# Gathered pairs added at every fourth unit of products, and count groups stored without gaps, in a three-layer graph kernel

## The chip, the cores and the metric

The kernel runs on one core of one Trainium2 chip. The metric is device time in microseconds (us), the median over runs of the same program. A profile is one further execution, with every instruction and every DMA packet recorded.

## What is computed

The input is a graph of 2500 nodes with 256 features each and 80000 edges (src, dst), sorted by dst. After a layer norm and a relu come three layers of edge convolution, and their outputs, joined, go through one more matrix:

```python
def _edge_conv(x, src, dst, W, b):
    xi = x[dst]
    xj = x[src]
    m = jnp.concatenate([xi, xj - xi], axis=-1) @ W + b
    s = jax.ops.segment_sum(m, dst, num_segments=N)
    cnt = jax.ops.segment_sum(jnp.ones((dst.shape[0],), m.dtype), dst, num_segments=N)
    return s / jnp.maximum(cnt, 1.0)[:, None]
...
h = jnp.maximum(_layernorm(x, axis=-1), 0.0)
xs = [h]
for W, b in ((W0, b0), (W1, b1), (W2, b2)):
    h = jax.nn.relu(_edge_conv(h, src, dst, W, b))
    xs.append(h)
return x + jnp.concatenate(xs, axis=-1) @ Wf + bf
```

The sum over the edges of a node can be written as a product with a matrix of counts: entry (s, d) is the number of edges from node s to node d. The kernel builds that matrix on the chip and multiplies with it, once per layer.

## The kernel before, in words

The nodes lie in NT = 20 tiles of 128. The columns of the count matrix (the destination nodes) are cut into windows of W = 6 nodes, and the windows into NG = 5 groups: four of 80 windows (480 columns) and a last one, group 4, of 78 windows (468 columns). FEW = 112 destination nodes, which fit in no window, are treated apart, by gathering their edges' rows one by one.

**The count groups.** One group is a tile `a` of 128 partitions x 20 node tiles x 480 columns (`new_a`, L796), in one of two pools, by the group's parity. So two groups at a time are in the on-chip memory. In layer 0, `build` (L835) fills a group from compared keys while the products of the group before run; `finish` (L847) then stores it to `a_dram[g]` in DRAM. Group 4 uses 468 of the tile's 480 columns, so that each of its 20 rows in a partition is followed by a gap of 48 bytes, on the chip and in DRAM, and its store (L850) and its load (L856) move 20 rows of 1872 bytes per partition. The other groups have no gap. Layers 1 and 2 load with `load_a` (L853) the groups that are no longer there.

**Layers 1 and 2** (L1054 to L1090). First `nodes_split` (L754) makes `z`, the node features times a part of the weights, as a high and a low half (`zh`, `zl`) for TensorE and as a whole in DRAM (`z_dram`). Then the five groups follow, in the order 4, 3, 2, 1, 0 in layer 1 and 0 to 4 in layer 2. For each group:

- `final` (L778) is called for the node tiles that the group touches: products with a part of Wf into one of four PSUM banks, and one VectorE addition into `acc`.
- `layer` (L932) yields after each of its 24 units of TensorE work, u = 0 to 23: 20 units of four products of `zh` or `zl` with the counts (L947), and then four units of own products (L951). ScalarE takes the result at the end (L954).
- After the group, `load_a` is called for the group two places further in the order, into the buffer that has just been read. So there are three loads in each layer, and group 4 is loaded once, in layer 2, after the third group, for use as the fifth.

**The gathered pairs.** For the FEW nodes, 60 gathers per layer fetch 128 rows of `z_dram` each, with an index per partition. `gather_pairs` (L902) is a generator over k = 0 to 33. Step k issues the two gathers of pair k on GpSimd's queue, into one of four buffers (`room`, L885), and adds pair k - 4 to `sums` on VectorE. The addition of pair k - 4 stands behind the gathers of that pair, and pair k + 1 can only be gathered once that addition has freed a buffer. The first call runs k = 0 to 3; each later `next(few)` runs one k.

Before the change, `next(few)` is called at the units u = 4, 6, ..., 18 of each group (L1079): eight per group, k = 4 to 11 in the first one. The 30 steps are used up in the fourth group.

**What sets the order.** Engines run side by side, but each runs its own instructions in the order of the program (helpers whose names end in "o" keep that order, and are all recorded at L280). A `next(few)` inside a group thus puts its addition on VectorE behind the `final` additions of that group and ahead of those of the next one. On GpSimd's queue the gathers share the order with the additions of x to `acc` (`add_rest`, L768, layer 1 alone). The loads stand on SyncE's queue (SP).

Of the kernel before, what the change touches and what calls it, by code (L numbers as in the profile page):

```python
# [8 lines left out]
F32 = mybir.dt.float32  # L9
# [256 lines left out]
F32R = mybir.dt.float32r  # L266
# [20 lines left out]
def run(it):  # L287
    for _ in it:
        pass
# [22 lines left out]
def by_windows(ctx: ExitStack, tc: tile.TileContext, x, src, dst, Ws, bs, Wf, bf, out, missing):  # L312
    nc = tc.nc
    PE, DVE, ACT, POOL, SP = nc.tensor, nc.vector, nc.scalar, nc.gpsimd, nc.sync
    PEo, DVEo, POOLo, ACTo, SPo = (InOrder(tc, e) for e in (PE, DVE, POOL, ACT, SP))
    P = 128
    N, D = x.shape
    E = src.shape[0]
    NT = (N + P - 1) // P
# [5 lines left out]
    W = 6  # L325
# [17 lines left out]
    GWS = []  # L343
    while sum(GWS) < NW:
        GWS.append(min(80, NW - sum(GWS)))
    G = max(GWS) * W
    GS = 480
    NG = len(GWS)
# [11 lines left out]
    dram = ctx.enter_context(tc.tile_pool(name="wdram", bufs=1, space=DRAM))  # L360
# [39 lines left out]
    cnt_few = const.tile([P, FEW], F32R, name="cnt_few")  # L400
    mine = const.tile([P, W], F32, name="mine")
    most = const.tile([P, 1], F32, name="most")
    a_dram = [dram.tile([P, NT, G], F32, name=f"a_dram{g}") for g in range(NG)]

    apools = [ctx.enter_context(tc.tile_pool(name="apool0", bufs=1))]
    pre = ctx.enter_context(ExitStack())
# [25 lines left out]
    def load_wb(l, queue=SP):  # L432
        ws[l] = wpool.tile([P, DC, D], F32, name="wt"), wpool.tile([P, DC, D], F32, name="wb", bufs=1)
        queue.dma_start(ws[l][1], Ws[l][D:2 * D, :].rearrange("(c p) d -> p c d", p=P))

    def load_wt(l, queue=SP):
        queue.dma_start(ws[l][0], Ws[l][0:D, :].rearrange("(c p) d -> p c d", p=P))

    def load_wf(l, queue=SP):
        wfs[l] = wpool.tile([P, DC, D], F32, name="wf", bufs=1)  # L440
        queue.dma_start(wfs[l], Wf[l * D:(l + 1) * D, :].rearrange("(c p) d -> p c d", p=P))
# [22 lines left out]
    def load_b(l, queue=SP):  # L464
        queue.dma_start(brow[PAD:PAD + 1, l % 2, :], bs[l].rearrange("(o d) -> o d", o=1))
# [288 lines left out]
    def nodes_split(l, t, zf):  # L754
        pz = bank()
        for c in range(DC):
            PE.matmul(pz[:, :D], hT[:, c, t * P:(t + 1) * P], ws[l][1][:, c, :],  # L757
                      start=(c == 0), stop=(c == DC - 1))
        sc = share[:, t:t + 1]
        if t == NT - 1:  # L760
            DVEo.scalar_tensor_tensor(zf, pz[:, :D], sc, brow[:, l % 2, :], op0=OP.mult, op1=OP.add)
        else:
            ACT.activation(zf, pz[:, :D], AF.Copy, scale=sc)
        SPo.dma_start(z_dram[l][t * P:(t + 1) * P, :], zf)
        DVEo.tensor_copy(zh[:, t, :], zf)
        DVEo.tensor_sub(zl[:, t, :], zf, zh[:, t, :].bitcast(F32))

    def add_rest(ts):  # L768

        a, b = ts[0], ts[-1] + 1  # L770
        DVEo.tensor_add(acc[:, a:b, :], acc[:, a:b, :], bf_sb.unsqueeze(1).to_broadcast([P, b - a, D]))
        yield
        full = min(b, NT - 1)
        POOLo.dma_start(acc[:, a:full, :], xr[:, a:full, :], accum_op=OP.add)
        if b == NT:
            POOLo.dma_start(acc[:LAST, NT - 1, :], x[(NT - 1) * P:N, :], accum_op=OP.add)

    def final(l, t):  # L778
        po = bank()
        for c in range(DC):  # L780
            PE.matmul(po[:, :D], hT[:, c, t * P:(t + 1) * P], wfs[l][:, c, :],  # L781
                      start=(c == 0), stop=(c == DC - 1))
        DVEo.scalar_tensor_tensor(acc[:, t, :], po[:, :D], share[:, t:t + 1], acc[:, t, :], op0=OP.mult, op1=OP.add)
        if l == L:
            n = P if t < NT - 1 else LAST
            SP.dma_start(out[t * P:t * P + n, :], acc[:n, t, :])


    def group_of(g):
        return FEW + sum(GWS[:g]) * W, GWS[g] * W  # L790

    def touched(g):
        c0, n = group_of(g)
        return [t for t in range(NT) if (t + 1) * P > c0 and t * P < c0 + n]

    def new_a(g):  # L796
        return apools[g % 2].tile([P, NT, GS], F32R, name="a")

    windows = [(g, s, min(BW, GWS[g] - s)) for g in range(NG) for s in range(0, GWS[g], BW)]
    ones_of = {}  # L800
# [46 lines left out]
    def finish(g, a):  # L847
        c0, n = group_of(g)
        ACTo.copy(a[PAD:PAD + 1, NT - 1, :n], cnt[PAD:PAD + 1, c0:c0 + n])
        SP.dma_start(a_dram[g][:, :, :n], a[:, :, :n].bitcast(F32))  # L850
        yield

    def load_a(g):  # L853
        a = new_a(g)
        n = group_of(g)[1]
        SP.dma_start(a[:, :, :n].bitcast(F32), a_dram[g][:, :, :n])  # L856
        return a

    def by_count(g):
# [20 lines left out]
    def add_sums(n):  # L880
        while n > 1:
            n //= 2
            DVEo.tensor_add(sums[:, :n, :], sums[:, :n, :], sums[:, n:2 * n, :])
# [6 lines left out]
    def rooms(l):  # L890

        for _ in range(AHEAD):
            two = room()
            yield two[:, 0, :]
            yield two[:, 1, :]
        for i in range(SUMS):
            yield sums[:, i, :]
        for _ in range(AHEAD):
            yield hot.tile([P, BW * CH, NB], BF16, name="one_n", bufs=AHEAD).rearrange(
                "p k m -> p (k m)")[:, :2 * D].bitcast(F32)  # L900

    def gather_pairs(l):  # L902

        got = []
        for k in range(EDGES // 2 + PAIRS):
            if k >= PAIRS:
                if k == PAIRS + 1:
                    DVEo.tensor_add(sums[:, :2, :], got[0], got[1])
                elif k > PAIRS:
                    DVEo.tensor_add(sums[:, :2, :], sums[:, :2, :], got[k - PAIRS])  # L910
            if k < EDGES // 2:
                two = room()
                got.append(two)
                for i in range(2):
                    POOLo.indirect_dma_start(
                        out=two[:, i, :], out_offset=None, in_=z_dram[l][:, :],
                        in_offset=bass.IndirectOffsetOnAxis(ap=who[:, 2 * k + i:2 * k + i + 1], axis=0))
            if k >= PAIRS - 1:
                yield
# [12 lines left out]
    def layer(l, g, a, own, PE=PE, ACT=ACT):  # L932

        c0, n = group_of(g)
        pa = ps_agg.tile([P, DC, 512], F32, name="pa")
        ways = [(o, c) for o in range(DC) for c in range(DC)]
        units = [(0, k) for k in range(NT)]
        for i, u in enumerate(own):
            units.insert(u + i, (1, i))
        last = {}  # L940
        for kind, i in units:
            last.update({o: (kind, i, o) for o in (range(DC) if kind == 0 else ways[i][:1])})
        for kind, i in units:
            if kind == 0:
                for o in range(DC):
                    for z in (zh, zl):
                        PE.matmul(pa[:, o, :n], z[:, i, o * P:(o + 1) * P], a[:, i, :n],  # L947
                                  start=(i == 0 and z is zh), stop=(z is zl and last[o] == (kind, i, o)))
            else:
                o, c = ways[i]  # L950
                PE.matmul(pa[:, o, :n], ws[l][0][:, c, o * P:(o + 1) * P], hT[:, c, c0:c0 + n],  # L951
                          start=False, stop=(last[o] == (kind, i, o)))
            yield
        ACT.activation(hT[:, :, c0:c0 + n], pa[:, :, :n], AF.Relu)  # L954
# [8 lines left out]
    a = new_a(0)  # L963
# [55 lines left out]
    for g in range(NG):  # L1019
# [26 lines left out]
        if g + 1 < NG:  # L1046
            run(finish(g + 1, a1))
            held, a = a, a1
# [5 lines left out]
    for l in range(1, L):  # L1054
        groups = list(range(NG))
        if l % 2:
            groups.reverse()


        last = [t for t in touched(groups[0]) if t]  # L1060
        for t, zf in zip([t for t in range(1, NT) if t not in last] + last + [0], rooms(l)):
            nodes_split(l, t, zf)
        few = gather_pairs(l)
        next(few)
        if l + 1 < L:
            load_b(l + 1)
            load_wb(l + 1)
            load_wt(l + 1)
        finished = []
        for j, g in enumerate(groups):  # L1070
            now = [t for t in touched(g) if t not in finished]
            for t in now:
                final(l, t)
            finished += now
            rest = add_rest(now) if l == 1 else None
            if j == NG - 1:
                load_wf(l + 1)
            for u, _ in enumerate(layer(l, g, tiles[g], LATE)):
                if 4 <= u < NT and u % 2 == 0:  # L1079
                    next(few, None)  # L1080
                if rest and u in (1, NT):
                    next(rest, None)
            if j == 1 and l + 1 < L:
                DVEo.tensor_sub(ws[l + 1][0], ws[l + 1][0], ws[l + 1][1])
            if j + 2 < NG:
                del tiles[g]
                tiles[groups[j + 2]] = load_a(groups[j + 2])
        run(few)
        add_sums(2)
        layer_few(l)  # L1090
# [41 lines left out]
```

## Time and profile before

| | |
|---|---|
| median of 3 runs | 551.21 us (550.27 to 553.93) |
| the profiled execution, its own time | 549.29 us |
| its span, first to last instruction | 547.6 us |
| TensorE busy | 511.1 us, 93% of the span |
| VectorE, ScalarE, GpSimd busy | 263.9, 136.3, 261.3 us |
| mean granted TensorE clock | 0.964 |
| gathers of pairs (`one_m<-z_dram,who`) | 120, 979 ns each on GpSimd |
| additions of pairs (`sums<-sums,one_m`) | 56, 692 ns each; 118.8 us of waiting for gathers before them |
| loads of a count group (`a<-a_dram`) | five of 4800 KB, one of 4680 KB |

PE is TensorE, PEld its weight loads, DVE VectorE, ACT ScalarE, POOL GpSimd, SP SyncE. In the chain of waits, each row is a start, a length and the work (or the wait) that held up the end of the kernel. "issue" is time in which the engine waited for nothing that the profile shows. The granted clock is the share of its full rate that TensorE was given.

The stages in the span: preparation to 61 us, layer 0 with the building of the counts to 205 us, layer 1 to 357 us, layer 2 to 524 us, the last `final` products to the end.

### The profile page before, as it was taken

The numbers are of one execution on the slowest core, as the hardware profiler recorded it, in microseconds if no ns is written. First come the engines' busy times: TensorE is split into PE (matmuls) and PEld (weight loads), VectorE is DVE, ScalarE is ACT, GpSimd is POOL, SyncE is SP. The second block draws the span as 40 slices with busy tenths as digits, with TensorE's granted clock in tenths as the row PEclk, the third lists the DMA queues.
The fourth block names the chain that finished last, engine by engine and source line by source line (L and its number), as shares of the span: only waits on it lengthen the run. The fifth ranks groups of instructions, "written<-read, shape, count | busy, mean of one in ns | idle before, by whom it ended". The sixth has DMA issues, their size and how long they took to land.

```text
span 547.6 us, 7491 instructions
## 1 busy us (share of the span) xinstructions
PE 511.1 (93%) x2875; PEld 415.1 (76%) x2875; DVE 263.9 (48%) x556; ACT 136.3 (25%) x310; POOL 261.3 (48%) x243
## 2 busy tenths in 40 slices
PE   8999999999999999994999999999939999984996
PEld 4888887888888888882778787788817787854875
DVE  7999888898888126621332122356213231211033
ACT  6666675547343205100000000042000000000000
POOL 4782278878788800277564534002762755400000
PEclk9999999999999999996899999999968999996999
DMA  8238759979996597333989999523337588994023
GB/s 277 70 97 156 132 220 304 395 112 342 144 274 181 87 271 255 111 105 102 368 267 300 143 344 120 91 96 116 105 105 310 171 261 201 181 154 160 1 78 115
DMA packets 42547, 100.29 MB, mean 183 GB/s; under 512 B 4663, under 2 KB 36870, under 8 KB 41350
## 3 DMA queue, kind: packets, MB, share of 16 engines
q1 hardware_dynamic: 22310, 68.78, 33.4%
q0 software_dynamic: 19264, 29.84, 32.7%
q10 hardware_dynamic: 928, 1.11, 0.7%
q8 instruction: 24, 0.39, 0.3%
q14 instruction: 21, 0.17, 0.1%
HBM read 62.21 MB, written 37.50 MB: 182 GB/s over the span
## 4 chain that ended last, share of the span: by engine, by line
PE 85%; DMA 9%; issue 4%; DVE 1%; ACT 0%; SPq 0%; DVEq 0%; ACTq 0%
PE pa L947 29%; PE pa L280 20%; PE bank L781 9%; PE bank L280 9%; DMA a<-a_dram 7%; PE bank L757 6%; PE pz L280 6%; PE pa L951 5%; DMA wf<-in_L_gnn_Wf_dram 2%; PE turned L280 1%; DMA dst_i<-in_dst_dram 1%; DVE one_n L280 0%; DVE one_m L280 0%; ACT hT L280 0%; DVE acc L280 0%
## 5 line engine op out<-in xcount | busy, mean ns | idle before, releaser
L280 POOL DMA_INDIRECT one_m<-z_dram,who x120 | 117.5, 979 | 150.0 <-DVE acc L280 65.4
L947 PE MATMUL pa<-a,zh 128*128 128x480 f32 (+1 forms) x400 | 156.1, 390 | 11.8 <-DMA a<-a_dram 9.4
L947 PE MATMUL pa<-a,zl 128*128 128x480 f32 (+1 forms) x400 | 153.8, 385 | 0.4 <-issue 0.4
L280 POOL DMA_INDIRECT sums<-z_dram,who x60 | 100.2, 1670 | 25.3 <-issue 17.1
L280 DVE TENSOR_TENSOR sums<-sums,one_m 128x512 f32<-128x512 f32 x56 | 38.8, 692 | 123.0 <-DMA one_m<-z_dram,who 118.8
L947 PEld LDWEIGHTS pa<-a,zh 128*128 128x128 f32 x400 | 76.7, 192 | 25.5 <-issue 12.9
L947 PEld LDWEIGHTS pa<-a,zl 128*128 128x128 f32 x400 | 76.6, 192 | 13.2 <-issue 0.9
L280 PE MATMUL pa<-a,zh 128*128 128x480 f32 (+1 forms) x200 | 81.6, 408 | 0.0
L280 DVE TENSOR_TENSOR one_m<-iota_m,key_m 128x1024 bf16<-128x1024 bf16 x100 | 68.8, 688 | 17.5 <-PE bank L280 15.4
L954 ACT ACTIVATE hT<-pa 128x960 f32<-128x960 f32 (+1 forms) x10 | 9.7, 968 | 271.2 <-PE pa L951 205.5
L280 PE MATMUL pa<-a,zl 128*128 128x480 f32 (+1 forms) x200 | 75.8, 379 | 0.0
L280 DVE SCALAR_TENSOR_TENSOR acc<-bank,share,acc 128x256 f32<-128x256 f32 x60 | 27.5, 481 | 81.2 <-PE bank L781 81.2
L280 ACT CAST a<-bank 128x480 fp32r<-128x480 f32 x100 | 51.4, 564 | 58.9 <-PE bank L280 53.9
L280 DVE TENSOR_TENSOR one_n<-iota_n,key_n 128x960 bf16<-128x960 bf16 x100 | 65.2, 652 | 0.0
L781 PE MATMUL bank<-wf,hT 128*128 128x256 f32 x240 | 56.5, 387 | 9.0 <-issue 8.5
L781 PEld LDWEIGHTS bank<-wf,hT 128*128 128x128 f32 x240 | 46.6, 194 | 18.9 <-issue 12.5
L280 PEld LDWEIGHTS <-one_m 128*128 128x128 bf16 x796 | 43.3, 98 | 8.9 <-issue 3.3
L280 PE MATMUL bank<-one_n,one_m 128*128 128x120 bf16 x796 | 49.0, 216 | 0.2 <-ACT junk L280 0.2
L280 PEld LDWEIGHTS pa<-a,zh 128*128 128x128 f32 x200 | 37.7, 188 | 8.5 <-issue 3.0
L951 PE MATMUL pa<-hT,wt 128*128 128x480 f32 (+1 forms) x80 | 37.7, 605 | 6.8 <-issue 6.8
L280 PEld LDWEIGHTS pa<-a,zl 128*128 128x128 f32 x200 | 37.6, 188 | 7.0 <-issue 2.1
L757 PE MATMUL bank<-wb,hT 128*128 128x256 f32 x160 | 34.9, 379 | 0.0
(145 smaller groups left out, 413.3 us busy)
## 6 DMA issues: line engine op xcount, KB each, us to landing
a<-a_dram SPq DMA_DIRECT2D x5, 4800.0 KB
a_dram<-a SPq DMA_DIRECT2D x4, 4800.0 KB
a_dram<-a SPq DMA_DIRECT2D x1, 4680.0 KB
a<-a_dram SPq DMA_DIRECT2D x1, 4680.0 KB
out_dram<-acc SPq DMA_DIRECT2D x19, 128.0 KB, 1.7
z_dram<-one_m SPq DMA_DIRECT2D x16, 128.0 KB, 3.4
z_dram<-sums SPq DMA_DIRECT2D x16, 128.0 KB, 3.6
acc<-in_x_dram POOLq DMA_DIRECT2D x4, 512.0 KB
```

Source lines behind the costliest of these rows:

```text
L280: return self.tc.keep_in_program_order(call(*args, **kwargs))
L757: PE.matmul(pz[:, :D], hT[:, c, t * P:(t + 1) * P], ws[l][1][:, c, :], start=(c == 0), stop=(c == DC - 1))
L781: PE.matmul(po[:, :D], hT[:, c, t * P:(t + 1) * P], wfs[l][:, c, :], start=(c == 0), stop=(c == DC - 1))
L947: PE.matmul(pa[:, o, :n], z[:, i, o * P:(o + 1) * P], a[:, i, :n], start=(i == 0 and z is zh), stop=(z is zl and last[o] == (kind, i, o)))
L951: PE.matmul(pa[:, o, :n], ws[l][0][:, c, o * P:(o + 1) * P], hT[:, c, c0:c0 + n], start=False, stop=(last[o] == (kind, i, o)))
L954: ACT.activation(hT[:, :, c0:c0 + n], pa[:, :, :n], AF.Relu)
```

## The change

Three places, and no other line:

```diff
-    a_dram = [dram.tile([P, NT, G], F32, name=f"a_dram{g}") for g in range(NG)]
+    a_dram = [dram.tile([P, NT, n * W], F32, name=f"a_dram{g}") for g, n in enumerate(GWS)]
...
     def new_a(g):
-        return apools[g % 2].tile([P, NT, GS], F32R, name="a")
+
+        n = group_of(g)[1]
+        a = apools[g % 2].tile([P, NT * GS], F32R, name="a")
+        return a[:, :NT * n].rearrange("p (t n) -> p t n", n=n)
...
-        SP.dma_start(a_dram[g][:, :, :n], a[:, :, :n].bitcast(F32))
+        SP.dma_start(a_dram[g], a.bitcast(F32))
...
     def load_a(g):
         a = new_a(g)
-        n = group_of(g)[1]
-        SP.dma_start(a[:, :, :n].bitcast(F32), a_dram[g][:, :, :n])
+        SP.dma_start(a.bitcast(F32), a_dram[g])
         return a
...
             for u, _ in enumerate(layer(l, g, tiles[g], LATE)):
-                if 4 <= u < NT and u % 2 == 0:
+                if u % 4 == 1:
                     next(few, None)
```

For groups 0 to 3 the tile and its place in DRAM are what they were. In group 4 a row of 468 columns now follows the one before it directly, so a partition holds 37440 bytes in one piece. `next(few)` is now called at u = 1, 5, 9, 13, 17 and 21: six per group, k = 4 to 9 in the first, and the 30 steps are used up exactly at u = 21 of the fifth group.

## The prediction

> **What bounds the kernel now.** I read the page first: TensorE is busy for 93% of the span, and the chain is TensorE for 85%, a DMA for 9%, "issue" for 4%.
>
> ```profile
> span 547.6 us, 7491 instructions
> ...
> PE 511.1 (93%) x2875; PEld 415.1 (76%) x2875; DVE 263.9 (48%) x556; ACT 136.3 (25%) x310; POOL 261.3 (48%) x243
> ...
> PE 85%; DMA 9%; issue 4%; DVE 1%; ACT 0%; SPq 0%; DVEq 0%; ACTq 0%
> ```
>
> So only time in which TensorE stands can be won. The chain in order of time says where it stands:
>
> ```profile
> 249.12 1.56 issue
> 250.68 0.38 PE bank L781
> 251.05 1.78 issue
> ...
> 261.11 0.82 issue
> 261.93 19.28 PE pa L947 x80
> ...
> 397.68 1.56 issue
> ...
> 442.83 17.59 PE pa L947 x80
> 460.44 39.30 DMA a<-a_dram
> 499.74 0.14 issue
> 499.87 19.28 PE pa L947 x80
> ```
>
> Three places. Place C is the load of group 4 in layer 2, issued at 460.44, landed at 499.74; the waits say "PE pa L947 <- DMA a<-a_dram: 9.4". Places A (249.1 to 261.9, layer 1) and B (397.7 to about 413.3, layer 2) are no wait for data: TensorE goes on, but its instructions come singly, 0.7 to 2.8 us apart, with "issue" between. The busy times by stretch show both sides:
>
> ```profile
> core 0: us, PE busy (x) PEld busy (x) DVE busy (x) ACT busy (x) POOL busy (x), PEclk, DMA share, GB/s
> 227.90:248.50 20.60, 20.60 (x91) 16.94 (x90) 5.91 (x8) 0.00 (x0) 15.72 (x17) 1.00 0.34 96
> 248.50:262.00 13.50, 4.18 (x10) 2.16 (x9) 0.69 (x1) 0.00 (x0) 9.86 (x10) 0.62 0.43 106
> ...
> 413.50:428.00 14.50, 14.50 (x62) 12.10 (x62) 4.61 (x8) 0.97 (x1) 6.22 (x6) 0.93 0.93 375
> 443.00:459.00 16.00, 16.00 (x75) 13.66 (x74) 4.33 (x8) 0.91 (x1) 8.12 (x8) 1.00 0.94 335
> 460.40:499.90 39.50, 30.09 (x126) 23.09 (x124) 9.36 (x18) 1.94 (x2) 11.37 (x12) 0.93 0.90 182
> ```
>
> Ten products in the 13.5 us of A, 91 in the 20.6 us before. The loads of whole rows (413.5 and 443) move 375 and 335 GB/s, with gathers beside them; the load with gaps only 182 with gathers beside it.
>
> What do A and B share? GpSimd's timeline: in both, the first group's stream of gathers, back to back at 1.25 us.
>
> ```profile
> 227.91 0.99 POOL L280 DMA_INDIRECT one_m<-z_dram,who  x1 [36.39 <-DVE acc L280]
> ...
> 257.12 0.94 POOL L280 DMA_INDIRECT one_m<-z_dram,who  x1 [0.30 <-issue]
> ...
> 379.33 1.08 POOL L280 DMA_INDIRECT one_m<-z_dram,who  x1 [29.02 <-DVE acc L280]
> ...
> 408.34 0.95 POOL L280 DMA_INDIRECT one_m<-z_dram,who  x1 [0.30 <-issue]
> ```
>
> Each stream has 24 gathers (pairs 0 to 11). A ends 3.9 us after the last of them (261.9 against 258.06), B 4.0 us after (413.3 against 409.29). The beginnings are less alike, at gather 17 in A and 15 in B. The later stream of 16, from 420 to 440, shows no such place (20.50 us of TensorE in 20.50). I take the stalls to hang on a long stream of gathers and to end with it. That is an inference from two cases; the profile names no releaser.
>
> **The skill.** "DMA: Bandwidth & Descriptors", section "Queues, rings and completion order", says that each DMA engine goes round its queues a packet at a time. That agrees with place C: between 466 and 492, with gathers running, all DMA moves 163 GB/s, and from 493, after the last gather, 307. One short row of 1872 bytes per turn, against a gather's packet, is a poor share; a whole row per turn is a good one. "TensorE: Matmul & The Clock Gate", section "Part 1: The HAM clock gate", says that an idle window of about 3.4 us takes TensorE to half rate until a busy window has passed. The trace agrees: the clock is 0.62 in A, and the 80 products after C take 19.28 us against 17.04 for the same shapes at 227.64. I found no page on instructions that come 0.7 us apart. "SBUF — State Buffer", section "Operand start alignment", allows any fp32 start at a multiple of four bytes and times none.
>
> **The change, part by part.** *1. Load without gaps.* It removes the wait of 9.41 us and the half-clock restart, 19.28 - 17.04 = 2.24: **11.65 us**. The cover: TensorE needs group 4 at 490.47 (499.87 - 9.41), 30 us after the issue. 4680 KB are 4.79 MB; at the slower of the two rates, 335 GB/s, that is 14.3 us, landed by 475; at half of that rate it would still land at 489. The wait is back below 4.79 MB / 30.0 us = 160 GB/s. The gathers beside it lose: the pairs of the fourth group stand behind whole rows for some 15 us, as at 445.52 to 459.72, where VectorE waits 12.28 us for a pair. What is late next is VectorE; it must be through the additions of one group when TensorE comes to the `final` of the group after the next, since four banks carry the four `final` tiles between. That is a group, 24 us, of lag; the largest before is 323.86 - 308.68 = 15 us. So it is covered. The store in layer 0 (184.7) has no reader before layer 2: nothing.
>
> *2. Shape of the group's rows.* The 80 products of group 4 in each layer read rows that begin at multiples of 1872 instead of 1920 bytes. No row of the trace shows it. Best 0; worst, an estimate, a tenth of 3 x 17.04 = 5 us. A gain has no reason. I take 0.
>
> *3. Fewer additions per group.* Same 60 gathers at 979 ns and the same additions at 692 ns; none is on the chain, so moving them costs nothing directly while TensorE covers them. Of what they pass: on POOL, at u = 21, one pair follows layer 1's x addition, two DMAs at most, 2.44 us; on DVE, the step at u = 1 now stands ahead of the bias addition (1.49 us at most), for which only that x addition waits, and nothing of layer 1 reads its result. SP's queue is not touched. The last group had no pair and gets six: four have been gathered, two more cost 4 x 1.25 us and some 3 us to land; they begin at about 337 in layer 1 and are added by 348, before the few nodes' products at 357; layer 2 has 30 us. Covered.
>
> *4. The stream of the first group.* Six steps instead of eight: 20 gathers, 4 x 1.25 = 5.0 us shorter. If A and B end with it, each is 5.0 us shorter, less what TensorE did in that time: in A about 2.5 products of 0.22 (0.5 us), in B about 2.8 of 0.40 (1.1 us). Gain 4.5 + 3.9 = **8.4 us**. Bounds: 0, if the stalls have another cause, and all of it. In A: 13.2 us with seven products' worth of 1.5, and 1.7 of half clock after it (19.28 against 17.57), so 13.4. In B, 397.3 to 414.6, 17.3 us, with 3.6 of work: 13.7. Together 27 us.
>
> Sum on the profiled execution: 549.29 - 11.65 - 8.4 = 529.2. The median of the runs lies 1.9 above that execution: **531.1 us**.
>
> **Rivals.** *The stalls are not the gathers'.* Two stalls only, with beginnings at different gathers, and 60 gathers in layer 0 without one (at 1.67 us, with accumulation) speak for it; the ends speak against. Then only 11.65: 539.6 us. *They go altogether*, if the stall needs more than some 20 gathers, or the pairs that pile up unadded after the last addition of the group. The stall at gather 15 to 17 speaks against. 551.21 - 11.65 - 27.1 = 512.5 us. *The load is not joined* into one piece per partition: 551.21 - 8.4 = 542.8 us. Against it: the loads of 480 columns, written as three dimensions too, already run at 335 to 392 GB/s. *Slower:* the stall counts gathers in flight, and gathers held behind a whole-row load count. Every one of the eight later groups now has a stream of 12; with one stall of 3.2 us in each, 25.6 us, against at most 20.05 won, the time is 551.21 - 20.05 + 25.6 = 556.8. It decides from 20.05 / 8 = 2.5 us per group. Against it: streams of 16 beside loads show nothing before.
>
> **How the numbers follow.** Both parts as summed 0.42; stalls as before 0.27; stalls gone 0.15; load not joined 0.06; slower 0.06; the remaining 0.04 for a wait that only moves, near no change. I give the time of the first. The likeliest one's own range is 524 to 536 (5 us for the row starts above, some 7 for a half clock that falls otherwise or a stall that begins later below). For 8 in 10 the range reaches from the stalls gone to the load not joined: 512 to 544. What a measurement of this kernel can tell is 1%, 5.5 us: faster is all below 545.7. That takes the first four cases, 0.90; no change 0.05; slower 0.05.
>
> **What would show it.** In the profile of the changed kernel: the load of group 4 in layer 2 lands within 20 us and TensorE has no wait on it (step 1); the products of 468 columns stay at 0.21 us apart (step 2); no `sums` wait reaches the few nodes' products (step 3); the first streams have 20 gathers, and the "issue" places end about 4 us after them (step 4). I am wrong if the places A and B keep their length, or if TensorE waits for VectorE's `acc` additions.

## The result and the profile after

The changed kernel takes 532.48 us (median of 4 runs, 531.97 to 533.3) against 551.47 us beside it: ratio 0.965, 95% interval 0.962 to 0.969. The prediction was 531.1 us. The sum came out right, and four of its terms did not: one cost was missed, two gains were mis-sized, and one gain, seen in later runs alone, was held to be nothing.

The page of the changed kernel, its span, its busy times and its chain:

```profile
span 531.6 us, 7489 instructions
...
PE 506.9 (95%) x2875; PEld 414.1 (78%) x2875; DVE 264.6 (50%) x556; ACT 136.0 (26%) x310; POOL 268.9 (51%) x243
...
PE 66%; POOL 14%; DMA 14%; issue 4%; DVE 1%; ACT 0%; SPq 0%; POOLq 0%; ACTq 0%
```

GpSimd is now in the chain with 14%, and it was not there before. The waits of TensorE tell why:

```profile
PE pa L280 <- DVE sums L280: 9.1, 1, 9.1
PE pa L953 <- issue: 4.5, 5, 1.5
...
PE bank L781 <- issue: 1.5, 2, 0.9
PE pa L949 <- issue: 0.7, 2, 0.3
```

The wait of 9.4 us for the load of group 4 is gone, and the "issue" waits of places A and B are down from 8.5 + 6.8 + 2.7 = 18.0 us to 6.7. The same lines before:

```profile
PE bank L781 <- issue: 8.5, 6, 1.8
PE pa L951 <- issue: 6.8, 6, 2.4
PE pa L947 <- issue: 2.7, 3, 1.6
```

But a wait of 9.1 us for `sums` is new: it is the few nodes' product at the end of layer 0. (Lines of the changed kernel stand two lower: L949 is the L947 of before.) The chain in order of time, from the end of layer 0 through place A:

```profile
193.50 17.73 DMA sums<-z_dram,who
...
213.72 2.47 PE pa L280 x10
216.19 18.36 PE bank L757 x80
234.55 4.32 PE bank L781 x20
238.87 17.00 PE pa L949 x80
...
261.17 0.59 issue
261.75 0.47 PE bank L781
262.23 0.92 issue
...
264.56 17.62 PE pa L949 x79
```

The last gather of layer 0 took 17.73 us to land. Layer 1's first product starts at 238.87, and started at 227.64 before. Place A is there still, but only from 261.2 to 264.6. Cut at the same products, the two spans compare so (us, worked out from the starts of the groups' products; the columns on the right are a later pair of profiles, `e9_before` and `e8_after`, taken on two chips and told of below):

| stretch | before | after | difference | before, later run | after, later run | difference |
|---|---|---|---|---|---|---|
| to the first product of layer 1 | 227.64 | 238.87 | +11.23 | 231.94 | 237.67 | +5.73 |
| to the end of its second group's products (place A) | 53.57 | 43.31 | -10.26 | 40.37 | 40.27 | -0.10 |
| to the first product of layer 2 | 99.33 | 99.33 | 0 | 107.29 | 99.33 | -7.96 |
| to the first of its second group (place B) | 38.04 | 32.72 | -5.32 | 24.25 | 24.25 | 0 |
| to the first of its last group (place C) | 81.29 | 71.89 | -9.40 | 89.29 | 71.88 | -17.41 |
| to the end | 47.73 | 45.48 | -2.25 | 47.76 | 45.40 | -2.36 |
| span | 547.6 | 531.6 | -16.0 | 540.9 | 518.8 | -22.1 |

### The profile page after: what moved, and what is told of

The parts are those of the page before. It is cut to its first block, busy times and chain, and to the rows that moved or that the text cites. A ratio compares the mean times of both kernels' runs of the same rounds, so it can differ in the third digit from the quotient of the medians.

```text
span 531.6 us, 7489 instructions
## 1 busy us (share of the span) xinstructions
PE 506.9 (95%) x2875; PEld 414.1 (78%) x2875; DVE 264.6 (50%) x556; ACT 136.0 (26%) x310; POOL 268.9 (51%) x243
## 4 chain that ended last, share of the span: by engine, by line
PE 66%; POOL 14%; DMA 14%; issue 4%; DVE 1%; ACT 0%; SPq 0%; POOLq 0%; ACTq 0%
PE pa L949 33%; POOL sums L280 14%; PE bank L781 10%; DMA sums<-z_dram,who 10%; PE bank L757 7%; PE pa L953 6%; PE pz L280 6%; PE bank L280 2%; DMA wf<-in_L_gnn_Wf_dram 2%; PE pa L280 1%; DMA z_dram<-zl 1%; DMA z_dram<-zh 1%; DMA dst_i<-in_dst_dram 1%; PE turned L280 1%; DVE sums L280 0%
## 5 line engine op out<-in xcount | busy, mean ns | idle before, releaser
L280 POOL DMA_INDIRECT one_m<-z_dram,who x120 | 121.1, 1009 | 168.8 <-DVE sums L280 53.3
L949 PE MATMUL pa<-a,zh 128*128 128x480 f32 (+1 forms) x400 | 153.9, 385 | 0.3 <-issue 0.3
L949 PE MATMUL pa<-a,zl 128*128 128x480 f32 (+1 forms) x400 | 151.9, 380 | 0.3 <-issue 0.3
L280 POOL DMA_INDIRECT sums<-z_dram,who x60 | 104.2, 1737 | 24.7 <-issue 17.4
L949 PEld LDWEIGHTS pa<-a,zl 128*128 128x128 f32 x400 | 75.1, 188 | 13.2 <-issue 1.2
L949 PEld LDWEIGHTS pa<-a,zh 128*128 128x128 f32 x400 | 75.1, 188 | 12.8 <-issue 0.5
L280 PEld LDWEIGHTS pa<-a,zh 128*128 128x128 f32 x200 | 37.7, 188 | 8.5 <-issue 3.0
L280 PEld LDWEIGHTS pa<-a,zl 128*128 128x128 f32 x200 | 37.6, 188 | 7.0 <-issue 2.1
L953 PE MATMUL pa<-hT,wt 128*128 128x480 f32 (+1 forms) x80 | 35.4, 573 | 4.6 <-issue 4.5
L757 PE MATMUL bank<-wb,hT 128*128 128x256 f32 x160 | 36.0, 388 | 0.0
```

The costliest lines, as they stand in the source:

```text
L280: return self.tc.keep_in_program_order(call(*args, **kwargs))
```

## The experiments

Two theories stood after the first comparison. One: the store of group 4 in whole rows holds up the last gathers of layer 0 (+11.2), and the long gather streams make places A and B, which the new pacing shortens by 15.6. The other: the late start of layer 1 comes from the pacing or from the moment of the store, and A and B have some other cause. The runs that follow fell on four chips, one set of runs on each, and in each set the kernel before was timed beside them. Which chip the first comparison had is not on record.

**The two parts alone.** The kernel before with the new pacing, and the changed kernel with the old one:

```diff
-                if 4 <= u < NT and u % 2 == 0:
+                if u % 4 == 1:
```

> The kernel before with the new pacing alone (u = 1, 5, ..., 21); group 4 keeps its gaps. Theory (the store of group 4 without gaps holds up the gathers of layer 0 and costs 11.2 us at the start of layer 1; the shorter first streams win 10.3 us in place A and 5.3 us in place B): neither the loss at the start of layer 1 nor the gain of the load appears, the first product of layer 1 starts at about 227.6 as before, and the time is 551.5 - 15.6 = 536 us. Rival (places A and B win only the 8.4 us of the prediction, and the rest of what A won in the changed kernel belongs to the later start of layer 1): 551.5 - 8.4 = 543 us.

Measured: 530.08 us, ratio to before 0.976 (0.970 to 0.982); the kernel before took 544.32 us here.

```diff
-                if u % 4 == 1:
+                if 4 <= u < NT and u % 2 == 0:
```

> The changed kernel with the old pacing (u = 4, 6, ..., 18): only the gaps of group 4 are removed. Theory (the store in rows of 37440 bytes holds up the gathers of layer 0): TensorE waits some 9 us for the sums of layer 0, the first product of layer 1 starts at about 239, the load of group 4 wins 11.65 us, and on balance the time is 551.5 - 11.65 + 11.2 = 551 us. Rival (the wait in layer 0 has to do with something other than the shape of the group): no wait for sums, 551.5 - 11.65 = 540 us.

Measured: 530.27 us, ratio 0.974 (0.968 to 0.980). TensorE's waits in this second profile:

```profile
PE pa L280 <- DVE sums L280: 9.1, 1, 9.1
PE bank L781 <- DVE acc L280: 5.1, 1, 5.1
```

The wait for `sums` comes with the missing gaps, and with the pacing alone it is 2.2 us. That fits the first theory. The rest fits neither: there are no "issue" waits in either profile, even with the old pacing, and a wait for VectorE's `acc` stands where none had been. Each part alone wins some 14 us. The two gains overlap: with the pacing alone TensorE still waits 13.0 us for the load of group 4, and the kernel before, profiled again below, waits 17.4.

**Places A and B.** So the same programs had to be profiled in such a set of runs.

> The kernel before, once more, for its profile beside the three kernels of this call. In the first profile the semaphore updates of TensorE at the ends of products of 244.7 and 400.4 came only at 262.0 and 413.5, at the ends of places A and B; the four kernels of the call before had no such place. Theory (the places hang on the length of the gather stream alone): A and B are there again, some 13 us each, time about 551 us. Rival (they come and go with the chip or the execution, for the same program): A and B are absent here, and what the kernel before loses lies elsewhere, at the load with gaps and at VectorE's additions; about 544 us, as in the call before.

The kernel that ran under this label was the changed one. It gives 520.59 us, ratio 0.955 (0.952 to 0.958), beside the next one, the same kernel.

> The changed kernel, once more. Theory (the places hang on the length of the gather stream alone): A and B are there, 3 and 8 us long, 532 us, ratio 0.965. Rival (they come and go with the chip or the execution): without them the time is that of the kernel with the store in rows of 1872 bytes, 515.5 us, and what the wait for the sums is longer in the changed kernel (9.1 - 5.4 = 3.7 us), 519 us; the ratio to the kernel before at 544 is then 0.954.

Measured: 521.11 us, ratio 0.958 (0.955 to 0.961). No A, no B. And the kernel before itself:

> The kernel before, unchanged (the run e7_before was meant to be this one; the kernel sent there was the changed one). Theory (places A and B belong to the chip or the execution; on other chips the kernel before loses its time elsewhere): no A and B; TensorE waits some 13 us for the load with gaps, as with the new pacing alone, and some 5 us for VectorE's acc in the last group of layer 1, as with the gaps alone removed; about 544 us. Rival (A and B are in the program, and the new pacing or the missing gaps removed them): A and B are there with some 13 us each, and TensorE's semaphore updates come late at their ends.

Measured: 543.01 us (543 for the kernel beside it too). Its waits of TensorE:

```profile
PE pa L947 <- DMA a<-a_dram: 17.4, 1, 17.4
PE bank L781 <- DVE acc L280: 5.8, 1, 5.8
PE pa L280 <- DVE sums L280: 3.5, 1, 3.5
```

No A and B here either, with the same 24 gathers in the stream; the rival fell. In the four later sets of runs this kernel took 540 to 546 us, and in the first one 550 to 554. Whether it is the chip that makes the places, or something else in that set of runs, isn't settled. What they are can be read more closely, though. The load into group 4's buffer waits for the last product that reads it. The first profile of before, with TensorE's last product of group 4 and then SyncE's issue of the load:

```profile
244.31 0.37 PE L947 MATMUL pa<-a,zl 128*128 128x468 f32 x1
```

```profile
262.03 0.32 SPq L856 DMA_DIRECT2D a<-a_dram  x1
```

The same two in the later profile of the same kernel:

```profile
248.63 0.37 PE L947 MATMUL pa<-a,zl 128*128 128x468 f32 x1
```

```profile
249.03 0.32 SPq L856 DMA_DIRECT2D a<-a_dram  x1
```

In the later profile the load was issued 0.03 us after the product ended, in the first one 17.3 us after. The trace's records of semaphores (the counters by which engines signal each other) agree: TensorE's signals for products that ended at 244.7, 247.8, 248.7 and 253.4 all stand together, from 262.0 to 262.3. So in A and B it is not only that TensorE's instructions come singly: what TensorE has finished isn't known to the others. In the changed kernel's first profile it was 9.4 us in A (255.87 to 265.32) and 9.5 in B (399.1 to 408.61). In every later profile each such load is issued 0.03 us after its product. The late signals can also come without the gaps: in the first profile of before, the load behind the second group of layer 2 was issued at 442.83, 6.7 us after its product had ended, while TensorE ran on.

The two profiles with A and B have one thing more in common. Counted in the traces' semaphore records, they hold 2180 and 2261 arrivals of GpSimd's DMAs, where the twelve others hold 3173 to 3182. From 375 to 440 us, around B, it is 128 and 153, against 558 in the later profile of before. So signals also went unrecorded there. Whether the recording was disturbed by what made A and B, or had a part in making them, no run tells.

**The length of the stream.** In a set of runs without A and B the stream was also made shorter and longer.

```diff
-                if u % 4 == 1:
+                if u % 3 == 1 and j > 0:
```

> The changed kernel with no step in the first group of a layer (a stream of 8 gathers instead of 20) and steps at u = 1, 4, 7, ... in the other four. Theory (a long stream of gathers holds TensorE's semaphore updates back): where the changed kernel has A and B, they vanish here and about 11 us are won, 521 us against 532; where it has none, the two kernels are within 3 us. Rival (A and B are not the gathers'): they stay, no difference.

Measured: 539.02 us, ratio 0.991 (0.987 to 0.994): 18 us slower than the changed kernel beside it, where 3 at most was expected. The last pairs come too late in layers 1 and 2:

```profile
PE pa L280 <- DVE sums L280: 19.8, 3, 9.2
```

The changed kernel beside it has one such wait, of 7.9 us, in layer 0. Here there is one in each layer (9.2, 6.3 and 4.3 us). VectorE's last addition of a pair in layer 1 begins at 359.76, and the few nodes' product at 360.97, 6.3 us late. No theory had asked how near the end the last pairs are: in the changed kernel's first profile they are added by 356.2, and the product needs them at 358.

```diff
-                if u % 4 == 1:
+                if u % 2 == 1 if j == 0 else u % 4 == 1:
```

> The changed kernel with ten steps in the first group (a stream of 28 gathers instead of 20), and the rest at every fourth unit. Theory (a long stream holds the updates back): where the changed kernel has A and B, they end some 10 us later here, each up to 10 us longer, 545 to 552 us against 532; where it has none, VectorE's additions stand one group earlier and nothing changes by more than 3 us. Rival (A and B are not the gathers'): no difference in either.

Measured: 527.84 us, ratio 0.969 (0.966 to 0.973), 7 us slower than the changed kernel, where again 3 at most was expected. (It has twelve steps in the first group and so 32 gathers; the expectation counted ten and 28.) Again no "issue" waits, but one of 4.5 us for `acc`. So on this chip streams from 8 to 32 gathers all leave TensorE's signals alone. What the two runs show is the window in which the additions must lie.

**The additions ahead of `acc`.** Eight steps per group again, spread over the group:

```diff
-                if u % 4 == 1:
+                if u % 3 == 1:
```

> The changed kernel with the steps at u = 1, 4, 7, ..., 22: eight per group as before the change, but spread over the whole group. Theory (what counts is how many additions of pairs stand on VectorE ahead of the next group's acc additions): the eight per group of the fourth group bring back the wait of TensorE for VectorE's acc at the end of layer 1, 4.5 to 5.1 us with 1 us of slow clock; ratio to the kernel before some 0.968, about 527 us where the changed kernel has 521. Rival (the bunching between u = 4 and 18 counts): no such wait, 521 us.

Measured: 527.67 us, ratio 0.972 (0.967 to 0.976), with a wait of 4.9 us for `acc`. Spreading doesn't help; the count does. It is the count over the layer, not that in one group: the kernel with 12 steps in the first group has six in the later ones, as the changed kernel has, and waits all the same. VectorE's timeline in the later profile of before, just ahead of the wait:

```profile
325.42 0.69 DVE L280 TENSOR_TENSOR sums<-sums,one_m 128x512 f32<-128x512 f32 x1 [2.98 <-DMA one_m<-z_dram,who]
328.72 0.69 DVE L280 TENSOR_TENSOR sums<-sums,one_m 128x512 f32<-128x512 f32 x1 [2.61 <-DMA one_m<-z_dram,who]
329.33 1.65 DVE L280 SCALAR_TENSOR_TENSOR acc<-bank,share,acc 128x256 f32<-128x256 f32 x4
```

The four `acc` additions belong to the `final` products of the fourth group, which ran from 299.6 to 302.9. They stand behind pairs that come one every 3.3 us, and behind 22 additions in all. TensorE wants their four banks a group, 24 us, later, for the fifth `final`, and gets them at 329.87; its work before them was done at 324.02. Counted in the traces, 22 additions stand ahead of these `acc` additions in the kernels that wait (before, old pacing, 32 gathers, every third unit: 329.3, 335.0, 332.9, 333.6), and 16 in those that don't (pacing alone and the changed kernel: 299.4, 306.3).

**The store.** First the size of its rows:

```diff
-        SP.dma_start(a_dram[g], a.bitcast(F32))
+        if g < NG - 1:
+            SP.dma_start(a_dram[g], a.bitcast(F32))
+        else:
+            for t in range(NT):
+                SP.dma_start(a_dram[g][:, t, :], a[:, t, :].bitcast(F32))
```

> The changed kernel with the store of group 4 issued as 20 DMAs of one row of 1872 bytes per partition, in place of one DMA of 37440 bytes per partition; group 4 still lies without gaps and its load is one piece. Theory (it is the size of the store's packets that takes the turns of the DMA engines from the gathers): the wait of TensorE for the sums at the start of layer 1 is gone and the time is 532.5 - 11.2 = 521 us. Rival (it is the amount of bytes, or the moment of the store): the wait stays, 532 us.

Measured: 515.52 us, ratio 0.947 (0.942 to 0.952); the wait for `sums` is 5.4 us, less than the changed kernel's 7.4 to 9.7 in its three later profiles, but not gone. Then its place, after layer 1's stores of z:

```diff
-        SP.dma_start(a_dram[g], a.bitcast(F32))
+        if g < NG - 1:
+            SP.dma_start(a_dram[g], a.bitcast(F32))
...
+        if l == 1:
+            SPo.dma_start(a_dram[NG - 1], tiles[NG - 1].bitcast(F32))
```

> The changed kernel with the store of group 4 issued after layer 1's z_dram has been stored, instead of at the end of layer 0. Theory (the store collides with the last gathers of layer 0): the wait for the sums at the start of layer 1 is gone, 532.5 - 11.2 = 521 us, unless the store now holds up the first gathers of layer 1; these are hidden while TensorE has products of its own, so this should cost nothing or shift place A. Rival (the store is not the cause): the wait stays, 532 us.

Measured: 513.08 us, ratio 0.947 (0.939 to 0.955). The wait at the start of layer 1 is gone, as expected; the one wait for `sums` that is left, 1.9 us, stands at the end of layer 1. The changed kernel takes 520 to 521 us in the later runs, so by medians short rows win 5 us and the late place 7, where both were expected to win 11. The DMA view of the 8 us from 191 to 199, when the gathers of layer 0 end, counts packets, MB and the share of 16 engines for each queue; q0 carries the gathers, q1 the store. The later profile of before, store in rows of 1872 bytes:

```profile
q0 software_dynamic: 511, 0.47, 58.3%
q1 hardware_dynamic: 537, 1.01, 37.6%
```

The changed kernel, `e8_after`, rows of 37440 bytes:

```profile
q1 hardware_dynamic: 85, 3.18, 93.2%
q0 software_dynamic: 93, 0.09, 8.3%
```

The changed kernel with the store in single rows:

```profile
q0 software_dynamic: 511, 0.47, 36.6%
q1 hardware_dynamic: 546, 0.91, 35.3%
```

And with the late store (`e12_late`), so that only gathers run:

```profile
q0 software_dynamic: 676, 0.61, 52.0%
```

In each of the first three the two queues send about as many packets as each other. That agrees with what the Trainium skill says in "DMA: Bandwidth & Descriptors", section "Queues, rings and completion order", of turns taken by packets; what the trace counts as the store's packets here are single rows. When they are 20 times as long, the gathers get a fifth of what they had (0.47 to 0.09 MB); with short rows they keep 0.47, of 0.61 that they reach alone. One DMA with short rows (before) and twenty of them give the same 0.47, so it is the size of the packets, as the theory had it, and not the number of DMAs.

But it is not the whole loss. Layer 1's first product starts at 227.14 with the late store, at 231.94 in the later profile of before, at 234.74 with single rows and at 236.57 to 239.53 in the three later profiles of the changed kernel. By these profiles, one for most kernels and not all on one chip, a store beside the last gathers costs some 5 to 8 us with short rows too, and 9 to 12 with long ones. So short rows could not win 11. (In the first profile of before layer 1 started at 227.64, with short rows and no wait for `sums`; why it differs isn't known.)

**The best version beside the changed kernel**, on one chip:

> The changed kernel beside the one with the late store, on one chip. Theory: without places A and B, ratio to the kernel before 0.957, some 520 us, with a wait of 8 to 10 us for the sums of layer 0. Rival (places A and B come back on this chip, as in the first profiles): 532 us beside 551 us.

Measured: 520.25 us, ratio 0.959 (0.956 to 0.963).

> The changed kernel with the store of group 4 after layer 1's z_dram. Theory (the store moved, and nothing held up in its new place): 8 us below the changed kernel on the same chip, some 512 us, the wait for the sums of layer 0 at 2 us and one of 2 us for the sums of layer 1. Rival (the 513 us of the first run were that chip's): less than 3 us below the changed kernel.

Measured: 513.3 us, ratio 0.946 (0.941 to 0.950): 7 us below the changed kernel, by medians, and the intervals don't touch. In its profile layer 0 has no wait for `sums`. The one of 1.0 us is that of the few nodes' product at the end of layer 1:

```profile
345.06 0.47 PE L280 MATMUL pa<-only,sums 128*128 128x112 f32 x2 [1.02 <-DVE sums L280]
```

So the late store wins 9.4 us up to layer 1's first product (227.14 against 236.57) and gives little back: it runs beside layer 1's first gathers while TensorE has products of its own, and from the last group of layer 1 to layer 2 it takes 1.2 us more (45.40 from product to product instead of 44.16).

## Why the prediction came out as it did

*Step 1, the load.* Right to the digit in the runs predicted for: -9.40 and -2.25, against 9.41 + 2.24. In the later pair it is worth 17.41 + 2.36 = 19.8 us. TensorE comes to group 4 30.0 us after the load is issued in both profiles of before. But in the later one, with no A and B, 17 gathers are still to come when the load is issued, and 12 in the first, so the load with gaps has gathers beside it for longer. It lands 47.30 us after its issue, where it took 39.30:

```profile
445.70 47.30 DMA a<-a_dram
```

The sentence "The store in layer 0 (184.7) has no reader before layer 2: nothing" is the step that failed. It asked who reads the store, and not who shares the DMA engines with it. The gathers of layer 0 did, with `sums` at the end of the layer behind them: the 0.47 MB that they moved in 8 us became 0.10 in the first pair too, and layer 1 began 11.23 us later (5.73 in the later pair, where the kernel before waited already). The view was at hand: place C had shown the same contest, with the gathers winning it, and a whole row per turn turns it round.

*Step 2, the row starts.* Right. The 80 products of group 4 take 16.95 to 17.00 us after, 17.04 before; the bound of 5 us was not needed.

*Step 3, fewer additions per group.* Moving the additions was put at nothing "while TensorE covers them", and step 1 said of VectorE's lag "So it is covered". Both held for the first pair, and for the first pair alone: there the fourth group's `acc` came at 323.86, and TensorE, late by A, wanted the banks at 332.9. Without A the same 22 additions make TensorE wait 5.8 us and take 5.57 us for the 16 products after it instead of 3.45, 7.96 us in all, and the new pacing wins that. The lag was read against a TensorE that stood 13 us in A; the cover was borrowed from a stall. That the last pairs come in time was right, but they were added by 356.2 instead of "by 348", some 2 us ahead of need. The last gather, issued at 347.36, was added at 355.46, where step 3 gave a gather some 3 us to land. The loads had ended by 327.1. An addition of x, 512 KB, was issued on the same queue ahead of the last six gathers; that it held them up isn't shown.

*Step 4, the stream of the first group.* A and B did shorten, by 10.26 and 5.32 us instead of 4.5 and 3.9, and they still end soon after the stream: in A the last gather ends at 261.8 and the place at 264.6, in B at 405.1 and 408.7. But that the stream makes them is not shown. The kernel before has the same stream without them in a later run, and shorter and longer ones don't bring them about. What else must be given, and whether the pacing or the later start of layer 1 shortened them, stays open, because no later run had them. The 16 gathers from 420 to 440, which the prediction took to show nothing, had late signals too (the load at 442.83). Why TensorE's signals stick isn't known either.

*The sum.* Predicted -11.65 - 8.4 = -20.05; measured in the first pair -11.65 + 11.23 - 15.58 = -16.0 on the profiled spans. A missed cost of 11.2 was met by a gain 7.2 larger than forecast; the other 3 us are between the profiled executions and the medians, which differ by 19.0. That the two nearly cancelled was luck. In the later runs the change is worth more (ratio 0.955 to 0.959), as a different sum: +5.7 for the store, -8.0 for `acc`, -19.8 for the load. Of the rivals, "slower" and "not joined" fell at once: no stretch of later groups grew, and the load's packets are whole rows.

The clock was read rightly. The Trainium skill, in "TensorE: Matmul & The Clock Gate", section "Part 1: The HAM clock gate", tells of half rate after an idle window. The new wait shows it: the 80 products behind it take 18.36 us after 9.1 us of waiting (18.87 after 7.9 in the later run), and 17.28 without one.

## What to carry to other kernels

When a DMA's rows are made longer, ask what runs beside that DMA at each place where it is issued, not only who reads its result: short packets beside long ones get turns, not bytes. A lag that a stall hides is not covered; work out each wait as if the other waits were gone. And where a stall has no releaser in the profile, profile the same program again, in another set of runs, before a price is put on it.

## What the runs showed of the hardware

- One program has different bounds in different sets of runs. Before: 551 us with A and B and a load wait of 9.4 us; 543 us with neither place, a load wait of 17.4 and one of 5.8 for `acc`.
- In the two profiles of one set of runs TensorE's signals arrived up to 17.3 us after the product, while its own instructions came on a grid of about 0.70 us (before, in B: products at 402.80, 404.21, 406.30, 409.10 and 410.50, that is two, three, four and two steps apart).
- A packet of 37440 bytes takes 1.40 us by the packet records, one of 1872 bytes about 0.08 in the store; with two queues busy, each got about as many packets as the other.
- Rows of fp32 that begin at multiples of 1872 bytes cost TensorE nothing beside multiples of 1920: 16.95 us against 17.04 for 80 products.
